# Who issues the copies of the second half of x: GpSimd in the source's order, or SP

## The chip, the cores and the metric

The kernel runs on one core of a Trainium2 chip. The core has five engines with an instruction stream each: TensorE (PE; its weight loads are shown as PEld), VectorE (DVE), ScalarE (ACT), GpSimd (POOL) and SyncE (SP), which only issues transfers. Transfers (DMAs) are issued by SP, ScalarE or GpSimd and carried out by 16 DMA engines that all of them share. The metric is device time in microseconds (us), the median of several runs; less is better.

## The reference, cut to what matters

Two layers of graph attention on x, 8 batches of 2048 nodes with 256 channels (float32), with one adjacency matrix of 2048 x 2048 integers. About one entry in 128 is set, and the diagonal always is, so a node has some 17 neighbours on average. After each layer the input is added and the rows are normalised.

```python
# layer 0, for each batch
h1, h2, h3 = x @ W1, x @ W2, x @ W3
e = leaky_relu(h1 @ h2.T, 0.2)
e = where(adj > 0, e, -1e12)
x = layernorm(x + relu(softmax(e) @ h3))
# layer 1, for each batch; q has 4 heads of 64 channels
q = x @ W
e = leaky_relu(e_src[:, None, :] + e_dst[None, :, :], 0.2)   # q against the vector a
e = where(adj > 0, e, -9e15)
x = layernorm(x + elu(softmax(e over the neighbours) @ q))
```

## The kernel before, in words

The kernel uses that the matrix is sparse. It never forms the 2048 x 2048 logits. It makes a list of neighbours for every node and gathers the neighbours' rows.

**Tables.** The 8 batches are two halves of four. For each half there is a table in DRAM, `xg[0]` and `xg[1]`, of 2048 rows with the four batches side by side (1024 floats, 4 KB a row), so that one gather by node number fetches the row of all four batches. The table is made by transfers from DRAM to DRAM: for `xg[0]` by four of 2 MB (L255), for `xg[1]` by eight of 1 MB (L955), each for half the nodes of one batch. A row of such a transfer is 1 KB.

**Setup.** SP loads the adjacency matrix in 16 pieces. VectorE numbers the set entries, SP writes them back to DRAM as `edges`; in the midst of this it issues the four transfers of `xg[0]`. The nodes are ranked by degree, so that each tile of 128 nodes has its own number of slots (neighbour places): `SLOTS`, from 12 to 38.

**Units.** A unit is one tile of one half in one layer. Layer 0 takes the 16 tiles of half 0 and then those of half 1, each from 12 slots up to 38; layer 1 has 32 units more. A unit of layer 0 has these steps:

- `list_job` gathers a tile's rows of `edges` (tile `nb`, 1 MB), and `neighbours` takes the neighbour numbers out of them on VectorE (MAX8 and MATCH_REPLACE8, L491 and L494); done once for each tile, during half 0;
- `before0` gathers the tile's own rows (`xo`), copies them (`xr`, by SP, L512) and makes `g` of them: transposes on TensorE, copies `xT` on ScalarE (L407), a projection on TensorE, copies `g` on ScalarE (L523);
- `chunk_job` gathers the neighbours' rows, one indirect DMA of 128 rows for a slot, two slots to a ring tile `s` (L191);
- `logits0` multiplies each row with `g` and sums on VectorE (L543, four for a slot), then the softmax;
- `sums0` scales the rows on ScalarE (L634, four for a slot) and adds them on TensorE (L612, four for a slot);
- `after0` projects, normalises and writes the row of layer 1's table (`qg`).

**Order.** Two things set it. The loop at the end of `fast_path` writes the program: for each unit it goes through the slots of `sums0`, and at each slot `tick` first lets `pump` issue gathers as long as ring tiles are free (`credits`, `RING` = 16), then moves the logits of later units, the list of a later tile and the ends of earlier units on by a step. After that a planner orders the instructions of each engine by its own costs and by what they wait for. From L339 on GpSimd is taken out of this (`manual_schedule`): its instructions stay in the order in which the source writes them. SP's don't: the planner may put a transfer of SP as early as its data allow. The eight transfers of `xg[1]` stand in the loop at the starts of the units 2 to 9 (L952 to L955).

An engine works through its stream in order: an instruction that waits holds up all behind it. The first instructions that read `xg[1]` are the gathers of unit 16.

Of the kernel before, what the change touches and what calls it, by code (L numbers as in the profile page):

```python
# [125 lines left out]
def fast_path(  # L126
# [24 lines left out]
    nc = tc.nc  # L151
    B, N, C = x.shape
    NT = N // P
    KC = C // P
    HB = B // 2
# [51 lines left out]
    xg = [tc.dram_tile([N, HC], F32, name=f"xg_{h}") for h in range(2)]  # L207
# [273 lines left out]
    def neighbours(t):  # L481
        K, o = SLOTS[t], offs[t]
        while t not in loaded:
            yield
        v = loaded[t]
        if t in up[:3]:
            numbered(v)
        rounds = -(-K // 8)
        m = sp.tile([P, 40], F32, tag="m", name=f"m_{t}")
        for i in range(rounds):  # L490
            nc.vector.max(m[:, ts(i, 8)], v)  # L491
            yield
            if i + 1 < rounds:
                nc.vector.match_replace(v, m[:, ts(i, 8)], v, 0.0)  # L494
                yield
        credits[0] += 1
        nc.vector.tensor_scalar(neg[:, o : o + K], m[:, :K], 0.5, LOWEST, ALU.is_lt, ALU.mult)
        far = sp.tile([P, 40], F32, tag="far", name=f"far_{t}", bufs=2)[:, :K]
        nc.vector.tensor_scalar(far, m[:, :K], 0.5, FAR, ALU.is_lt, ALU.mult)
        nc.vector.scalar_tensor_tensor(  # L500
            idx[:, o : o + K], m[:, :K], 1.0, far, ALU.subtract, ALU.add
        )
        listed[t] = True
# [416 lines left out]
    def finish(u):  # L920
        yield from after[u.layer](u)
# [6 lines left out]
    def tick(limit):  # L928
        pump()
        while late and late[0][0] <= clock[0]:  # L930
            late.popleft()[1]()
        for _ in range(2):
            if ahead[0] < limit:
                ahead[0] += next(stream, 0)
        for queue in queues:
            for _ in range(min(len(queue), 2)):
                if queue and next(queue[0], queue) is queue:
                    queue.popleft()
        clock[0] += 1
# [6 lines left out]
    for j, u in enumerate(units):  # L946
        begun = False
        if 0 < j and j + 2 < NT:
            lists.append(neighbours(up[j + 2]))
        while len(ends) > 1:  # L950
            tick(0)
        if 2 <= j < 10:  # L952
            b, half = divmod(j - 2, 2)
            n = ts(half, N // 2)
            nc.sync.dma_start(xg[1][n, ts(b, C)], x[HB + b, n])  # L955
        left = float(u.K)
        for share in sums[u.layer](u):
            ahead[0] -= share
            left -= share
            tick(left + units[min(j + 1, len(units) - 1)].K + LEAD)  # L960
            if not begun and left <= u.K / 2 and j + 3 < len(units):
                begun = True
                v = units[j + 3]
                starts.append(before[v.layer](v))
        ends.append(finish(u))
# [249 lines left out]
@with_exitstack  # L1215
def kernel(
    ctx: ExitStack,
    tc: tile.TileContext,
    x: bass.AP,
    adj: bass.AP,  # L1220
    w1: bass.AP,
    w2: bass.AP,
    w3: bass.AP,
    wq: bass.AP,
    a: bass.AP,
    out: bass.AP,
):
    nc = tc.nc
    flagp = ctx.enter_context(tc.tile_pool(name="flag", bufs=1))
    flag = flagp.tile([1, 1], I32, tag="flag", name="flag")  # L1230
    fast_path(tc, x, adj, w1, w2, w3, wq, a, out, flag)
    again = nc.values_load(
        flag, min_val=0, max_val=1, skip_runtime_bounds_check_because="a comparison gave it"
    )
    with tc.If(again > 0):
        general_path(tc, x, adj, w1, w2, w3, wq, a, out)
# [29 lines left out]
```

## Time and profile before

| what | before |
|---|---|
| median of three runs | 2865.22 us (2856.55 to 2866.15) |
| the profiled execution's own time | 2741.96 us |
| its span, first to last instruction | 2740.1 us |
| busy: PE, DVE, ACT, POOL | 1857.8, 2270.1, 1827.9, 1515.4 us |
| transfers of `xg[1]` (L955) | 8 of 1024 KB, issued by SP from 99.3 to 155.9 us |
| gathers of layer 0 (`s<-xg,idx`) | 602, from 126.4 to 1676.3 us, 1014 ns each (median) |
| logits of layer 0 (L543) | 2408 of 424 ns on DVE |
| scaling of rows, layer 0 (L634) | 2408 of 506 ns on ACT |

The profile is of one execution, which was shorter than the timed runs. A timeline row gives the start, the time taken, the engine, the line, the operation, what is written and read, how many instructions of a kind are put together, and, in brackets, how long the engine stood idle before it and what ended that. A row of SP has a "q": issuing is the work of its queue, and the time is that of the issue, not of the transfer. A GpSimd row of an indirect DMA is the time in which its descriptors are written; the rows land later.

### The profile page before, as it was taken

The page shows a single profiled execution, that of the slowest core. Times are in us where ns is not written, and L with a number is a line of the kernel's source. Part 1 is how long each engine was busy: PE and PEld are TensorE (multiplying, and loading weights), DVE is VectorE, ACT ScalarE, POOL GpSimd, SP SyncE. Part 2 cuts the span into 40 slices and gives each one's busy share as a digit, 9 for nine tenths or more (in the row PEclk, how much of TensorE's full clock was granted, in tenths as well). Part 3 has the DMA queues.
Part 4 walks back from the last instruction along what each step waited for, and adds up shares of the span by engine and source line. Part 5 has one row for each costly group of instructions (what it writes and reads, how often), then busy time and mean ns, then how long its engine had stood idle before and what let it go on. Part 6 is the DMA issues. An engine that isn't in the chain of part 4 may idle for free. (4 is left out here: it accounts for less than half of the span.)

```text
span 2740.1 us, 42566 instructions
## 1 busy us (share of the span) xinstructions
PE 1857.8 (68%) x12003; PEld 792.3 (29%) x12003; DVE 2270.1 (83%) x7247; ACT 1827.9 (67%) x4937; POOL 1515.4 (55%) x1506
## 2 busy tenths in 40 slices
PE   0148888888786866686878767756656667655763
PEld 0124434333332333343434323312221222211221
DVE  7679999999987876777787786788888888888996
ACT  6137787878879986867878779644445555554454
POOL 1353454545444544544454545577767777777773
PEclk9569999999988988898988888877877878877876
DMA  9996776777765566767686774899789998997892
GB/s 388 380 376 207 270 262 245 260 245 263 261 221 200 183 215 215 252 212 268 219 277 217 242 263 154 287 332 357 268 315 354 348 344 317 358 351 269 305 354 89
DMA packets 248036, 749.51 MB, mean 274 GB/s; under 512 B 55712, under 2 KB 73248, under 8 KB 241648
## 3 DMA queue, kind: packets, MB, share of 16 engines
q0 software_dynamic: 192064, 644.32, 66.5%
q1 hardware_dynamic: 54464, 101.21, 10.4%
q8 instruction: 98, 1.61, 0.2%
q10 hardware_dynamic: 1264, 1.18, 0.1%
q14 instruction: 146, 1.20, 0.1%
HBM read 721.50 MB, written 84.48 MB: 294 GB/s over the span
## 5 line engine op out<-in xcount | busy, mean ns | idle before, releaser
L612 PE MATMUL acc<-s,ident 64*64 64x512 f32 x9632 | 1336.4, 653 | 469.0 <-issue 285.4
L543 DVE CUSTOM_DVE_ANT_0 j<-s,g 128x256 bf16<-128x256 f32 x2408 | 1019.9, 424 | 199.1 <-DMA s<-xg,idx 133.0
L191 POOL DMA_INDIRECT s<-xg,idx x602 | 632.4, 1051 | 771.7 <-ACT s L634 280.9
L634 ACT ACTIVATE s<-s,e 128x256 f32<-128x256 f32 x2408 | 1000.1, 506 | 28.3 <-DVE e L569 27.4
L191 POOL DMA_INDIRECT s<-qg,idx x602 | 614.8, 1021 | 233.4 <-issue 123.7
L612 PEld LDWEIGHTS acc<-s,ident 64*64 64x64 f32 x9632 | 391.1, 144 | 1211.5 <-issue 777.6
L813 DVE TENSOR_TENSOR s<-s,p 128x2048 f32<-128x2048 f32 (+1 forms) x262 | 577.5, 2222 | 0.0
L809 ACT ACTIVATE s<-s,e 128x64 f32<-128x64 f32 x1472 | 357.8, 335 | 47.1 <-DVE e L777 35.8
L543 DVE DVE_READ_ACCUMULATOR2_ANT e<- 128x1 f32 x2408 | 197.0, 82 | 0.0
L696 PE MATMUL ps_q<-wqs,x1T 128*128 128x264 f32 x512 | 147.7, 426 | 35.9 <-ACT x1T L407 25.1
L199 POOL DMA_INDIRECT out_dram<-o,oidx x128 | 130.2, 1017 | 71.5 <-ACT o L395 36.7
L405 PE MATMUL ps_t_x<-ident,xo 128*128 128x128 f32 x256 | 56.7, 365 | 162.7 <-DMA xo<-xg,order 162.6
L383 ACT ACTIVATE z<-mv,roots 128x4 f32<-128x4 f32 x64 | 19.0, 297 | 212.2 <-DVE mv L373 212.1
L747 DVE TENSOR_TENSOR e<-s,own 128x32 f32<-128x32 f32 (+1 forms) x312 | 56.9, 186 | 104.0 <-DMA s<-qg,idx 97.6
L415 PE MATMUL ps_p_g<-A,xT 128*128 128x256 f32 x512 | 129.4, 399 | 8.9 <-DVE so L705 5.2
L415 PE MATMUL ps_p_h<-w_sb,hT 128*128 128x256 f32 x512 | 127.8, 392 | 1.4 <-ACT hT L407 1.4
L696 PEld LDWEIGHTS ps_q<-wqs,x1T 128*128 128x128 f32 x512 | 100.8, 206 | 88.4 <-ACT x1T L407 32.8
L395 ACT ACTIVATE o<-xr,nmr,rstd 128x256 f32<-128x256 f32 x128 | 66.3, 589 | 76.9 <-DVE nmr L391 67.3
L415 PEld LDWEIGHTS ps_p_g<-A,xT 128*128 128x128 f32 x512 | 96.7, 196 | 53.2 <-ACT s L634 8.1
L763 ACT ACTIVATE e<-e 128x304 f32<-128x304 f32 (+11 forms) x34 | 14.9, 439 | 143.7 <-DVE e L762 143.7
L491 DVE MAX8 m<-nb 128x8 f32<-128x2048 f32 x44 | 100.5, 2286 | 11.9 <-DMA nb<-edges,order 11.7
L415 PEld LDWEIGHTS ps_p_h<-w_sb,hT 128*128 128x128 f32 x512 | 92.0, 189 | 63.3 <-issue 17.9
(130 smaller groups left out, 1486.2 us busy)
## 6 DMA issues: line engine op xcount, KB each, us to landing
adj<-in_adj_dram SPq DMA_DIRECT2D x16, 1024.0 KB, 8.9
edges<-adj SPq DMA_DIRECT2D x16, 1024.0 KB, 19.8
xr<-xo SPq DMA_DIRECT2D x128, 128.0 KB, 6.9
x1s<-y SPq DMA_DIRECT2D x32, 512.0 KB, 7.3
xr<-x1s SPq DMA_DIRECT2D x32, 512.0 KB, 6.9
s<-xg,idx POOLq DMA_INDIRECT x602
s<-qg,idx POOLq DMA_INDIRECT x602
xg<-in_x_dram SPq DMA_DIRECT2D x4, 2048.0 KB
```

Source lines behind the costliest of these rows:

```text
L191: nc.gpsimd.indirect_dma_start(out=dst, out_offset=None, in_=table, in_offset=AT(ap=index, axis=0), bounds_check=table.shape[0] - 1, oob_i ...
L199: ins = nc.gpsimd.indirect_dma_start(out=table, out_offset=AT(ap=index, axis=0), in_=src, in_offset=None)
L395: nc.scalar.activation(dst[:, b, :], y[:, b, :], AF.Identity, bias=nmr[:, b : b + 1], scale=rstd[:, b : b + 1],)
L415: nc.tensor.matmul(pp[:, ts(j, C)], lhsT=srcT[:, ts((2 * i + j) * KC + k, P)], rhs=weight[:, k, :], start=(k == 0), stop=(k == KC - 1),)
L491: nc.vector.max(m[:, ts(i, 8)], v)
L543: nc.vector.tensor_tensor_reduce(out=jt, in0=rows[:, s, ts(b, C)], in1=u.g[:, ts(b, C)], scale=1.0, scalar=0.0, op0=ALU.mult, op1=ALU.add, ...
L612: nc.tensor.matmul(acc[r][64 * c : 64 * c + 64, :], lhsT=ident[rr, rr], rhs=rows[rr, s, c * 2 * w_ : (c + 1) * 2 * w_].rearrange("p (j w) ...
L634: nc.scalar.activation(v, v, AF.Copy, scale=u.p[i][:, b, k : k + 1])
L696: nc.tensor.matmul(pq[:, : C + 2 * H], lhsT=x1T[:, ts(i * KC + k, P)], rhs=w.wqs[:, k, :], start=(k == 0), stop=(k == KC - 1),)
L747: nc.vector.tensor_tensor(e[:, c * CHUNK : c * CHUNK + ns, :].rearrange("p s (b g) -> p s b g", b=HB), rows[:, :ns, :].rearrange("p s (b w ...
L809: nc.scalar.activation(v[:, a, g, :], v[:, a, g, :], AF.Copy, scale=pv[:, a, g : g + 1])
L813: nc.vector.tensor_tensor(v, v, pv.unsqueeze(3).to_broadcast([P, n * HB, H, D]), ALU.mult)
```

## The change

The eight transfers are issued by GpSimd instead of by SP. Their place in the source, their sizes, sources and destinations stay. GpSimd's instructions keep the source's order, so the transfers stand among its gathers where the loop writes them.

```diff
@@ -952,7 +952,8 @@
         if 2 <= j < 10:
             b, half = divmod(j - 2, 2)
             n = ts(half, N // 2)
-            nc.sync.dma_start(xg[1][n, ts(b, C)], x[HB + b, n])
+
+            nc.gpsimd.dma_start(xg[1][n, ts(b, C)], x[HB + b, n])
         left = float(u.K)
         for share in sums[u.layer](u):
             ahead[0] -= share
```

## The prediction

> **What bounds the kernel now.** I read the page first: the slices of each engine, then the DMA row.
>
> ```profile
> span 2740.1 us, 42566 instructions
> ...
> DVE  7679999999987876777787786788888888888996
> ...
> DMA  9996776777765566767686774899789998997892
> ```
>
> A slice is 68.5 us. The DMA engines are full in the first three; from the fourth on (205 us) VectorE is at 90% or more up to 750 us. So VectorE sets the pace of the first half of layer 0, and the start is another regime. The engines' busy time by stretch shows where one ends:
>
> ```profile
> 99.00:190.00 91.00, 20.98 (x71) 13.21 (x72) 63.72 (x141) 16.61 (x39) 40.78 (x40) 0.56 1.04 392
> 190.00:245.00 55.00, 45.73 (x254) 22.05 (x254) 50.76 (x222) 36.76 (x89) 24.71 (x23) 0.90 0.72 239
> 245.00:560.00 315.00, 269.06 (x1440) 127.25 (x1436) 304.23 (x1202) 245.96 (x603) 147.53 (x142) 0.94 0.73 254
> ```
>
> (Columns: stretch, length, busy time of PE, weight loads, DVE, ACT, POOL, then granted clock, DMA share, GB/s.) Up to 190 us the DMA share is 1.04; from 245 to 560 us it is 0.73 while DVE is busy 304 of 315. The changed transfers lie in the full stretch. This is SP's queue there:
>
> ```profile
> 99.30 41.97 SPq L955 DMA_DIRECT2D xg<-in_x_dram  x6
> 141.36 13.86 SPq L512 DMA_DIRECT2D xr<-xo  x4
> 155.26 12.06 SPq L955 DMA_DIRECT2D xg<-in_x_dram  x2
> ```
>
> All eight are issued between 99 and 168 us, long before their first reader (unit 16, whose first gather is at 801.8 us). What that costs VectorE is in its timeline:
>
> ```profile
> 154.66 2.29 DVE L491 MAX8 m<-nb 128x8 f32<-128x2048 f32 x1 [1.72 <-DMA nb<-edges,order]
> ...
> 180.31 2.29 DVE L491 MAX8 m<-nb 128x8 f32<-128x2048 f32 x1 [8.86 <-DMA nb<-edges,order]
> ...
> 190.24 0.43 DVE L543 CUSTOM_DVE_ANT_0 j<-s,g 128x256 bf16<-128x256 f32 x1 [2.92 <-ACT g L523]
> ...
> 192.63 0.43 DVE L543 CUSTOM_DVE_ANT_0 j<-s,g 128x256 bf16<-128x256 f32 x1 [1.38 <-ACT g L523]
> ```
>
> With 1.92 us before its first row of s at 136.64, VectorE idles 16.8 us between 121 and 193 us. After that, up to 560 us, its waits for DMAs add up to 0.2 us. So a microsecond saved on VectorE before 193 us moves all that follows, and the 16.8 us are all that can be had there.
>
> **What the Trainium skill says.** "DMA: Bandwidth & Descriptors", section "Issuing engines are not separate DMA queues": DMAs from any engine share the same 16 DMA engines. The trace agrees: with SP's transfers beside them, a gathered list issued at 166.50 is read only at 180.31, against 7.2 us from issue to use at 343.06. So the bytes don't get cheaper by moving; only their time of day changes. Same page, "Anatomy of one DMA": descriptor generation on GpSimd is "small, variable". No row of before has a plain DMA on POOL, so it can't be compared. "SBUF — State Buffer", section "SBUF: two separate sides": GpSimd can be locked out of writing descriptors by some VectorE operations; in the trace the gathers of rows stay near their median of 1014 ns (2240 at most), so I add nothing for it.
>
> **The change, part by part.**
>
> *Removed from SP:* eight issues, 54 us of SP's time (41.97 + 12.06); nothing that VectorE needs soon stands behind them. The copies xr<-xo that follow are read at 220 us; they come earlier, for no gain.
>
> *Removed from the DMA engines at 121 to 190 us:* 8 x 1 MiB. Between 121 and 131 us, when little else moves, the rate is 331 GB/s, so one transfer is 3.2 us of all engines and eight are 25.3 us. Step by step, with the order on the engines as it is:
>
> (a) The first row of s lands before VectorE is free (134.72): -1.92. (b) The list at 154.66: its 1.72 go too; together -3.64. (c) The list at 180.31:
>
> ```profile
> 166.50 1.08 POOL L191 DMA_INDIRECT nb<-edges,order  x1 [0.32 <-DMA s<-xg,idx]
> 168.11 0.99 POOL L191 DMA_INDIRECT xo<-xg,order  x1 [0.53 <-DMA s<-xg,idx]
> ...
> 343.06 1.02 POOL L191 DMA_INDIRECT nb<-edges,order  x1 [6.47 <-PE acc L612]
> ```
>
> POOL waited about 3.3 us for its own earlier gathers just before, so the list is issued near 163 and lands 7.2 us later, at 170, ten earlier. But VectorE then waits for g of unit 1, and that is set by ScalarE:
>
> ```profile
> 171.54 10.47 ACT L634 ACTIVATE s<-s,e 128x256 f32<-128x256 f32 x26 [0.77 <-DMA s<-xg,idx]
> 183.16 0.59 ACT L407 COPY xT<-ps_t_x 128x512 f32<-128x512 f32 x1 [1.15 <-PE ps_t_x L405]
> ...
> 189.62 0.59 ACT L523 COPY g<-ps_p_g 128x512 f32<-128x512 f32 x1 [3.02 <-PE ps_p_g L415]
> ```
>
> The 26 scalings end at 182.01 - 3.64 = 178.4. The copy xT, in order behind them, starts then and not at 183.16 (PE's transposes are done by then: xo lands near 172): -4.8. From there to g nothing changes (projection on PE, 6.5 us). So L543 of unit 1 starts some **5 us** earlier. That is what I take for the gain; it is bounded by 3.64 (if xo is no earlier) and 16.8 (if the planner, seeing other times, puts xT ahead of the scalings).
>
> *Added to POOL:* eight plain DMAs, in the source's order. Following the loop's credits and clock through the source gives POOL's order; it agrees with all 1,444 gathers and scatters of the two layers in the trace. By it the transfers stand after the instructions that end at 245, 285, 331, 371, 413, 463, 509 and 553 us. Cost of one on POOL: from below 1.0 us (a gather's row, 128 descriptors), from above 8 us (1,024 rows of 1 KB, eight times as many). I take 4. The cover: behind each, within five instructions, POOL idles waiting for ring buffers (12.05, 12.3, 6.5 and 4.0, 9.3, 11.7, 7.6, 7.5, 5.5 and 8.8 us), and in units 3 to 10 a gather ends at least 12 us, mostly over 20, before VectorE reads its row. A landing takes 4 to 7 us, so 8 us on POOL and 3.2 us of data are hidden: 0. Were both covers gone, they would cost 8 x (4 + 3.2) = 58 us.
>
> One place has no cover. The first transfer stands two instructions ahead of a list:
>
> ```profile
> 247.05 1.09 POOL L191 DMA_INDIRECT nb<-edges,order  x1 [0.30 <-ACT hs L647]
> ...
> 256.30 2.29 DVE L491 MAX8 m<-nb 128x8 f32<-128x2048 f32 x1
> ```
>
> From issue to use are 9.2 us, to landing some 7.4: 1.9 us to spare. The transfer adds its time on POOL with the gap of 0.3 and what of its 3.2 us of data isn't overlapped: 4.5 us (POOL 1.0) to about 8 (POOL 8). VectorE loses 2.6 to 6; or 0, if the planner, which knows POOL's new order, places that step later. At 343.06 and 166.50 too the step stands just behind the landing, so it seems to follow POOL's issue; I take 0 and keep 6 for the range.
>
> *Added to the DMA engines at 245 to 560 us:* 25.3 us in 315, so their share goes from 0.73 to 0.81: room. Each transfer goes through POOL's own queue, so gathers behind it wait 3.2 us; covered as above. POOL waits for the DMA eight before: a transfer has over 9 us (seven gathers of 1.3) to land. The gathers of unit 16 wait for the transfers, the last of which is done some 240 us before.
>
> *Sum:* -5 + 0 = -5, against the profiled execution's 2741.96 us (span 2740.1), 2737. The median of the runs is 2865.22, 4.5% more; scaled, -5 stays -5: **2860**.
>
> **The rivals.**
>
> *The whole stall goes.* For it: DMA share 1.04 exactly where VectorE idles. Against: ScalarE's 26 scalings stand ahead of xT. All 16.8 us, times 1.045: 2848.
>
> *Another order.* Only POOL's order is fixed; DVE, ACT, PE and SP follow a planner's costs. It gets other times for SP and POOL, and may order the rest otherwise to the end. Sensitive is the second half of layer 0 (913 to 1684 us), where rows arrive just in time: VectorE waits 115.8 us for s, PE 123.6 us for xo. A quarter of either is some 30 us: 2835 or 2895; half as much, 2850 or 2880, is as likely.
>
> *Slower: POOL's writing of descriptors.* From 245 to 560 us POOL is busy 147.5 us, and 142 gaps of 0.3 add 43: some 124 us are free for eight transfers, 15.5 each. Above that POOL is the bound; the lead of 12 to 20 us delays it by two units or so. At 25 us each, 8 x 9.5 = 76, less a lead of 17: +59, 2924. It decides from 16 us up. Against: that is twice the proportional price.
>
> *It doesn't move.* If POOL's transfers were placed at the start as SP's were, the time would stay 2865; POOL's order being the source's speaks against it.
>
> **How the numbers follow.** Small gain or none, as summed: 0.42. The whole stall gone: 0.19. Another order: 0.31 (faster 0.16, slower 0.11, near nothing 0.04). POOL bound: 0.06. Not moved: 0.02. A measurement tells about 0.5% (14 us) from no change. The stall gone counts as faster (17 us), so faster 0.35, same 0.48, slower 0.17. The likeliest case's own range is 2850 to 2868 (its gain from 3.64 to the 16.8 that bound it, less up to 6 for the list, and the 0.1% by which medians may differ); 8 in 10 takes in the stall gone and most of the reorderings: 2828 to 2884.
>
> **What would show it.** Right: no 1 KB traffic of SP after 99 us; the DMA share below 0.95 from 131 to 190 us; the two list waits (1.72, 8.86) gone; the first L543 of unit 1 near 185; eight plain DMAs on POOL from about 240 to 550 us; VectorE still 96% busy between. Wrong: a POOL row above 16 us, VectorE waiting for s or nb there, or, with the start 5 us earlier and these stages alike, a changed length of the stretch from unit 16 on: then the order did it.

## The result and the profile after

| kernel | median | range, runs |
|---|---|---|
| before | 2864.71 us | 2856.55 to 2869.58, 20 |
| after | 2864.61 us | 2857.77 to 2870.38, 20 |

The ratio is 1.0001, with a 95% interval from 0.9992 to 1.0009 (-2.3 to +2.6 us): no change that can be measured. The 5 us forecast did not come.

One thing has to be known for all that follows: the same kernel takes a different time on different occasions, 2741 to 2743 us on some and 2845 to 2865 us on others, and the profile on which the prediction was made belongs to the first kind, while the timing above and the profile after belong to the second. So each kernel is compared only with the kernel before timed on the same occasion, and for a like-for-like profile of both kernels the first experiment is used.

The page of the kernel after, by slices of 71.7 us:

```profile
span 2867.7 us, 42563 instructions
...
DVE  7668899998987876767787875777777678877886
...
DMA  9986787878665666677776757886788889887883
```

The third slice of the DMA row went from 9 to 8, and the sixth to eighth from 7, 6, 7 to 8, 7, 8: the bytes have moved to a later time. The engines' busy time by stretch in the kernel after (columns as before: PE, weight loads, DVE, ACT, POOL, then granted clock, DMA share, GB/s) says how much:

```profile
99.00:190.00 91.00, 16.18 (x61) 9.73 (x61) 63.40 (x141) 13.11 (x32) 41.31 (x41) 0.56 0.83 305
190.00:245.00 55.00, 46.05 (x253) 22.75 (x254) 45.84 (x195) 37.82 (x91) 21.28 (x21) 0.94 0.62 209
245.00:560.00 315.00, 265.22 (x1384) 124.35 (x1384) 295.52 (x1197) 241.91 (x593) 151.85 (x147) 0.92 0.77 269
```

From 1.04 to 0.83 in the stretch at the start, and from 0.73 to 0.77 after 245 us. Yet VectorE did no more work by 190 us than before (63.40 against 63.72 us busy), and less between 245 and 560 us (295.52 against 304.23). SP's queue in the kernel after has no 1 MiB transfer left there; only the copies xr<-xo follow the loading of the edges:

```profile
91.22 5.34 SPq L252 DMA_DIRECT2D edges<-adj  x3
121.02 106.39 SPq L512 DMA_DIRECT2D xr<-xo  x16
```

The instructions that touch x, in the kernel after (durations in ns, least, median and most, then the first and the last start):

```profile
L956 POOL DMA_DIRECT2D xg<-in_x_dram x8: 830/846/850, 249.2 to 566.4; - x8
```

Eight transfers on GpSimd, 0.85 us of its time each. And VectorE's timeline of the kernel after, in unit 0 and at the first logits of unit 1:

```profile
164.64 0.43 DVE L543 CUSTOM_DVE_ANT_0 j<-s,g 128x256 bf16<-128x256 f32 x1 [1.93 <-remote]
...
168.17 0.43 DVE L543 CUSTOM_DVE_ANT_0 j<-s,g 128x256 bf16<-128x256 f32 x1 [1.65 <-remote]
...
172.60 0.43 DVE L543 CUSTOM_DVE_ANT_0 j<-s,g 128x256 bf16<-128x256 f32 x1 [1.80 <-issue]
...
193.41 0.42 DVE L543 CUSTOM_DVE_ANT_0 j<-s,g 128x256 bf16<-128x256 f32 x1 [7.09 <-ACT g L523]
```

The two waits for lists (1.72 and 8.86 us) are gone, as forecast. But 11 logits of unit 0 now start late, by 0.2 to 1.9 us each, 11.8 us together. No DMA is named behind them; the rows of s that they read had landed by 147 us, and other logits of the same rows ran without a gap. "issue" and "remote" say that the profile shows no instruction of this core for which they waited; in the other six the row names only the VectorE instruction just before. I call them **late starts**. With them unit 0's logits end at 177.5 us (169.5 before), and unit 1 begins at 193.41 us instead of 190.24.

### The profile page after: what moved, and what is told of

Same layout as the page of the kernel before. It is cut to its first block, busy times and chain, and to the rows that moved or that the text cites. A ratio compares the mean times of both kernels' runs of the same rounds, so it can differ in the third digit from the quotient of the medians.

```text
span 2867.7 us, 42563 instructions
## 1 busy us (share of the span) xinstructions
PE 2106.8 (73%) x12003; PEld 902.8 (31%) x12003; DVE 2275.1 (79%) x7247; ACT 1833.3 (64%) x4937; POOL 1515.5 (53%) x1514
## 4 chain that ended last, share of the span: by engine, by line
PE 29%; DVE 26%; issue 17%; DMA 13%; ACT 10%; POOL 3%; another core or an unknown queue 1%; POOLq 0%; SPq 0%; DVEq 0%; ACTq 0%
PE acc L612 23%; DVE j L543 12%; ACT s L634 8%; DMA s<-xg,idx 4%; DMA s<-qg,idx 3%; DVE s L813 3%; DMA xo<-xg,order 3%; POOL s L191 3%; DVE m L491 2%; DVE e L543 2%; DVE nb L494 1%; PE ps_q L696 1%; PE ps_t_x L405 1%; PE ps_p_h L415 1%
## 5 line engine op out<-in xcount | busy, mean ns | idle before, releaser
L612 PE MATMUL acc<-s,ident 64*64 64x512 f32 x9632 | 1584.3, 667 | 372.9 <-issue 217.2
L612 PEld LDWEIGHTS acc<-s,ident 64*64 64x64 f32 x9632 | 499.2, 146 | 1247.7 <-issue 953.2
L415 PEld LDWEIGHTS ps_p_g<-A,xT 128*128 128x128 f32 x512 | 95.3, 194 | 53.4 <-ACT xT L407 10.4
L405 PEld LDWEIGHTS ps_t_x<-ident,xo 128*128 128x128 f32 x256 | 36.7, 180 | 209.1 <-issue 187.8
```

What stands on the lines that cost most here:

```text
L405: nc.tensor.transpose(pt[:, ts(j, P)], src[:, ts(4 * i + j, P)], ident)
L415: nc.tensor.matmul(pp[:, ts(j, C)], lhsT=srcT[:, ts((2 * i + j) * KC + k, P)], rhs=weight[:, k, :], start=(k == 0), stop=(k == KC - 1),)
L612: nc.tensor.matmul(acc[r][64 * c : 64 * c + 64, :], lhsT=ident[rr, rr], rhs=rows[rr, s, c * 2 * w_ : (c + 1) * 2 * w_].rearrange("p (j w) ...
```

## The experiments

All kernels were timed against the kernel before on the same occasion. The order of the instructions on PE, DVE and ACT in the kernel after is, instruction by instruction, that of the kernel before; the same holds for all kernels below but the one with doubled transfers on POOL, where a few of the 7,247 DVE instructions stand elsewhere.

| occasion | before (runs) | kernel | ratio | 95% interval |
|---|---|---|---|---|
| A | 2864.71 (20) | after | 1.0001 | 0.9992 to 1.0009 |
| B | 2742.57 (26) | before again | 1.0007 | 0.9998 to 1.0017 |
| B | | after | 0.9970 | 0.9958 to 0.9982 |
| B | | transfers left out | 0.9967 | 0.9954 to 0.9980 |
| B | | transfers twice, on SP | 1.0091 | 1.0078 to 1.0104 |
| C | 2861.52 (50) | late on SP | 1.0025 | 1.0015 to 1.0035 |
| C | | one unit later on POOL | 0.9987 | 0.9978 to 0.9996 |
| C | | transfers twice, on POOL | 1.0013 | 1.0003 to 1.0024 |
| D | 2845.32 (33) | transfers left out | 0.9999 | 0.9988 to 1.0011 |
| D | | one unit later on POOL | 0.9970 | 0.9958 to 0.9983 |
| D | | late on SP | 1.0007 | 0.9996 to 1.0019 |
| E | 2741.00 (11) | after | 0.9975 | 0.9962 to 0.9987 |

**Both kernels again (occasion B).** No edit.

> The kernel before once more, for a profile beside the others' and for what two timings of one kernel differ by. Every theory: ratio to before 1.000, within 0.001. If the 2741.96 us of the first profile was particular to that execution, this profile's own time is near 2865 us; the idle time of VectorE in 99 to 193 us is then read anew, and the 8.86 us wait for a list and the 1.72 us one should stand again.

> The changed kernel once more, on the same chip as the kernel before. Theory 1 (VectorE's idle time at the start is only refilled by something later in the same stretch, so nothing is gained and nothing is given back): ratio 1.000 within 0.001, first L543 of unit 1 at 190 us or later. Theory 2 (5 us are gained at the start and given back between 245 and 560 us): ratio 1.000, first L543 of unit 1 near 185 us, and VectorE about 5 us less busy than before's in 245 to 560 us.

The kernel after is faster here: 0.9970, that is 8.3 us (4.9 to 11.5). VectorE's timeline of the kernel before on this occasion:

```profile
158.56 2.29 DVE L491 MAX8 m<-nb 128x8 f32<-128x2048 f32 x1 [2.26 <-DMA nb<-edges,order]
...
181.54 2.30 DVE L491 MAX8 m<-nb 128x8 f32<-128x2048 f32 x1 [6.15 <-DMA nb<-edges,order]
...
189.41 0.43 DVE L543 CUSTOM_DVE_ANT_0 j<-s,g 128x256 bf16<-128x256 f32 x1 [0.85 <-ACT g L523]
```

And of the kernel after:

```profile
170.36 2.29 DVE L491 MAX8 m<-nb 128x8 f32<-128x2048 f32 x1 [2.87 <-DMA nb<-edges,order]
...
182.70 0.43 DVE L543 CUSTOM_DVE_ANT_0 j<-s,g 128x256 bf16<-128x256 f32 x1 [5.32 <-ACT g L523]
...
250.45 2.29 DVE L491 MAX8 m<-nb 128x8 f32<-128x2048 f32 x1 [2.25 <-DMA nb<-edges,order]
```

Neither has a late start in unit 0. Three things can be read. The second list is read at 170.36 us and not at 181.54. What holds VectorE then is g of unit 1, by 5.32 us, so the logits of unit 1 start 6.7 us earlier (7.5 against the first profile's 190.24) and not 11. And a list at 250.45 us makes VectorE wait 2.25 us where the kernel before had no wait. The cause of that wait stands in POOL's timeline of the kernel after:

```profile
237.15 0.85 POOL L956 DMA_DIRECT2D xg<-in_x_dram  x1
238.30 1.23 POOL L191 DMA_INDIRECT s<-xg,idx  x1 [0.30 <-PE ps_t_x L405]
239.83 1.06 POOL L191 DMA_INDIRECT nb<-edges,order  x1 [0.31 <-ACT x1T L407]
```

The list is two instructions behind the first transfer. It is used 10.6 us after its issue; in the kernel without transfers (below) 9.3 us were enough, without a wait.

ScalarE's timeline of the kernel after shows why g comes when it does:

```profile
167.57 10.48 ACT L634 ACTIVATE s<-s,e 128x256 f32<-128x256 f32 x26 [0.77 <-DVE e L569]
177.96 1.04 ACT L407 COPY xT<-ps_t_x 128x512 f32<-128x512 f32 x2
178.90 2.10 ACT L634 ACTIVATE s<-s,e 128x256 f32<-128x256 f32 x5
182.08 0.58 ACT L523 COPY g<-ps_p_g 128x512 f32<-128x512 f32 x1 [1.07 <-PE ps_p_g L415]
```

The 26 scalings stand ahead of xT, and xT starts the moment they end: 177.96 us, 5.2 earlier than in the first profile. Both copies of xT now follow each other, and g is copied 4.1 us after xT's start instead of 6.5. Against the first profile both things help. The kernel before on this occasion had the second of them already:

```profile
175.47 10.48 ACT L634 ACTIVATE s<-s,e 128x256 f32<-128x256 f32 x26 [0.78 <-DVE e L569]
185.86 1.04 ACT L407 COPY xT<-ps_t_x 128x512 f32<-128x512 f32 x2
```

Its g follows 3.0 us after xT. So what was gained here came from ahead of the scalings: the waits for the first row of s (4.3 us in this profile of before) and for the first list (2.26). The 6.15 us at the second list ran beside ScalarE's chain, which would have held unit 1 up anyway.

By the units' logits the lead is 6.7 us at the start of unit 1, 4.2 at the start of unit 4 (286.22 against 290.46), 4.7 at the start of unit 10 and 6.1 at the end of layer 0 (1679.0 against 1685.1). The rest of the 8.3 us is within what two executions of layer 1 differ by: 1053.9 in this profile of before, 1056.3 in the first one, 1049.9 in this one of after. So of the first two theories the second is right in kind, and wrong in that less is given back than gained.

**The transfers left out (occasion B).** The table of half 0 serves for both halves.

```diff
-    xg = [tc.dram_tile([N, HC], F32, name=f"xg_{h}") for h in range(2)]
+    xg = [tc.dram_tile([N, HC], F32, name="xg_0")] * 2
...
-            nc.sync.dma_start(xg[1][n, ts(b, C)], x[HB + b, n])
+            pass
```

> The eight transfers are left out altogether, and both halves read the one table, so half 1 of the output is computed from half 0's rows; all other instructions stay in their order. Theory 1: the transfers cost nothing in either place, ratio 1.000 within 0.001. Theory 2: the gain of the start without the price after it, 5 us less than before, ratio 0.998. The rival of the prediction in which the whole stall goes: 17 us less, ratio 0.994.

0.9967, or 9.1 us (5.5 to 12.6): as much as the kernel after, within the intervals. VectorE's timeline of this kernel:

```profile
168.85 2.29 DVE L491 MAX8 m<-nb 128x8 f32<-128x2048 f32 x1 [1.73 <-DMA nb<-edges,order]
...
181.14 0.43 DVE L543 CUSTOM_DVE_ANT_0 j<-s,g 128x256 bf16<-128x256 f32 x1 [5.28 <-ACT g L523]
```

With no transfer at all, unit 1 starts only 1.6 us earlier than in the kernel after, and g still costs 5.28 us. With this order of instructions that is what any placing of the transfers can bring at the start: some 8 us, not the 16.8 us of VectorE's idle time. At the end of layer 0 it leads by 7.8 us, the kernel after by 6.1.

**Each transfer twice, on SP (occasion B).** The second copy goes into a table that nobody reads.

```diff
-    xg = [tc.dram_tile([N, HC], F32, name=f"xg_{h}") for h in range(2)]
+    xg = [tc.dram_tile([N, HC], F32, name=f"xg_{h}") for h in range(3)]
...
-            nc.sync.dma_start(xg[1][n, ts(b, C)], x[HB + b, n])
+            [nc.sync.dma_start(xg[k][n, ts(b, C)], x[HB + b, n]) for k in (1, 2)]
```

> As the kernel before, but each of the eight transfers is issued twice by SP, the second time into a table that nobody reads: 16 MiB at the start in place of 8, some 25 us more of all DMA engines. If the DMA time at the start reaches the end of the kernel one for one, ratio 1.009 (25 us); if it does so only for what ScalarE's scalings don't cover (the 5 us of the prediction are the same again), 5 to 15 us, 1.002 to 1.005. Theory 1, with room still left at the start: ratio 1.000 within 0.001.

1.0091, or 25 us (21 to 29): the eight added transfers cost as much as the 25 us that their bytes take, while leaving out the first eight saved 9. VectorE's timeline of this kernel, at unit 2:

```profile
238.65 2.29 DVE L491 MAX8 m<-nb 128x8 f32<-128x2048 f32 x1 [24.64 <-DMA nb<-edges,order]
```

The list that VectorE needs at 214 us comes 24.64 us late. Why, SP's queue and POOL's timeline show:

```profile
161.29 50.58 SPq L955 DMA_DIRECT2D xg<-in_x_dram  x10
212.38 33.16 SPq L512 DMA_DIRECT2D xr<-xo  x12
```

```profile
224.31 0.99 POOL L191 DMA_INDIRECT xo<-xg,order  x1 [30.70 <-DMA xr<-xo]
...
230.79 0.99 POOL L191 DMA_INDIRECT nb<-edges,order  x1 [0.30 <-ACT xT L407]
```

SP's ten later transfers are issued until 212 us, and the copies xr<-xo stand behind them in SP's queue. POOL's next gather of xo waits 30.70 us for such a copy, and the list stands behind that gather in POOL's order. Once issued, it is read 7.9 us later, as fast as elsewhere. So the added transfers do reach the end of the kernel, but by the queue that they share with the copies; what 8 MiB more would cost at the start with nothing behind them in their queue was not run. In the kernel before on this occasion POOL waits 0.3 us for such a copy.

**The kernel before once more (occasion C).** No edit; one profile.

> A further profile of the kernel before. If it takes about 2742 us, it is the same as the earlier profile, L543 of unit 1 starting at 189 to 190 us and unit 3 ending near 290 us. If it takes about 2865 us, as both kernels did where the change was first timed, it decides between two readings of why nothing was gained there: either VectorE's stalls within unit 0 (11.3 us of waits without a cause on this core, in 99 to 330 us of the changed kernel's profile) stand in this kernel too, and unit 1 starts some 7 us later than in the changed kernel (near 200 us); or they don't, and it starts at about 190 us, which is no later than the 193.4 us of the changed kernel.

This one took 2859.62 us. VectorE's timeline of the kernel before on this occasion:

```profile
180.59 2.29 DVE L491 MAX8 m<-nb 128x8 f32<-128x2048 f32 x1 [9.31 <-DMA nb<-edges,order]
...
190.48 0.43 DVE L543 CUSTOM_DVE_ANT_0 j<-s,g 128x256 bf16<-128x256 f32 x1 [2.88 <-issue]
```

The second reading holds: unit 1 starts at 190.48 us, no later than the 193.41 us of the kernel after. There are no late starts in unit 0 here (there are in unit 3, 5.6 us), while the lists' waits stand, 1.77 and 9.31 us. The two waits together are 11.1 us, about what the late starts of unit 0 take in the kernel after (11.8).

**The transfers left out, where the kernel is slower (occasion D).** Same edit as above.

> The eight transfers left out again, both halves reading the one table, so half 1 of the output is computed from half 0's rows. Where the kernel before takes about 2742 us: 0.997 again, unit 1 starting near 181 us. Where it takes about 2861 us, the theory that VectorE's own late starts take the place of the waits for the lists says: the transfers cost nothing there at the start, ratio 0.999 to 1.001, unit 1 starting no earlier than 187 us, with 5 to 12 us of late starts inside unit 0. The rival, that POOL's transfers give back between 245 and 560 us what was gained: 0.996 or less there too, unit 1 starting near 181 us.

0.9999 (-3.4 to +3.1 us), where the same edit had saved 9.1 us on occasion B. VectorE's timeline of this kernel on occasion D:

```profile
163.32 0.42 DVE L543 CUSTOM_DVE_ANT_0 j<-s,g 128x256 bf16<-128x256 f32 x1 [0.96 <-DVE e L543]
...
166.14 0.43 DVE L543 CUSTOM_DVE_ANT_0 j<-s,g 128x256 bf16<-128x256 f32 x1 [0.97 <-DVE e L543]
...
170.79 0.20 DVE L566 TENSOR_REDUCE s<-e 128x4 f32<-128x48 f32 x1 [0.92 <-issue]
171.94 0.18 DVE L568 RECIPROCAL s<-s 128x4 f32<-128x4 f32 x1 [0.95 <-DVE s L566]
172.65 0.21 DVE L569 TENSOR_TENSOR e<-e,s 128x48 f32<-128x48 f32 x1 [0.53 <-DVE s L568]
...
186.88 0.42 DVE L543 CUSTOM_DVE_ANT_0 j<-s,g 128x256 bf16<-128x256 f32 x1 [7.10 <-ACT g L523]
```

Five logits of unit 0 start late, 3.9 us together, and six steps of its softmax too, some 3.1 us more than usual: 7.0 us, within the 5 to 12 expected. The softmax ends at 172.9 us, 5.7 later than without the transfers on occasion B (167.1), and from there to unit 1 it is 14.0 us in both. So unit 1 starts at 186.9 us, near the 187 named, and 3.6 us before the 190.5 of occasion C, not 8. With the transfers gone there is nothing that POOL could give back, and still nothing is gained. So a price of the transfers' new place is not needed to explain why nothing was gained when the change was first timed. It is not excluded to the microsecond: on this same occasion another kernel, below, gained 8.5 us for a reason that I don't know, so differences of that size between kernels are not all understood there.

**The transfers late, but on SP (occasions C and D).** Each waits for a 1 KB transfer of POOL into its own rows.

```diff
+            nc.gpsimd.dma_start(xg[1][half * (N // 2) : half * (N // 2) + 1, ts(b, C)], x[HB + b, half * (N // 2) : half * (N // 2) + 1])
             nc.sync.dma_start(xg[1][n, ts(b, C)], x[HB + b, n])
```

> The transfers stay on SP, but each waits for a 1 KB transfer of POOL into its own rows of the table, put where the changed kernel has its transfer; so SP moves the same bytes at the changed kernel's times. If only the time of day counts: 0.997 of the kernel before, as the changed kernel has, with L543 of unit 1 near 183 us, and unit 3 as long as in the changed kernel (43.0 us from its first L543 to its last). If POOL's queue counts, because gathers behind the transfer wait for its 3.2 us: unit 3 is 40.6 us, as in the kernel before, and 2 to 3 us more are gained. If the issuing engine is what gains: 1.000.

> SP moves the bytes at the changed kernel's times, as before. Where the kernel before takes about 2742 us: 0.996 to 0.997 if only the time of day counts; 1.000 if the issuing engine is what gains; above 1.001 if the wait that now stands in SP's queue holds up the copies behind it. Where it takes about 2861 us: 1.0025 again.

1.0025 and 1.0007. Both runs fell on occasions of the slower kind (on D leaving the transfers out gained nothing; on C it wasn't tried), so they can't tell whether the issuing engine or the time of day gains. That rival stays untested. Unit 3 takes 47.1 and 46.5 us against 47.6 in the kernel before, with late starts in each. No list waits near 250 us, which fits the reading that the wait comes from the transfer ahead of the list in POOL's own queue; but late starts would hide such a wait here. Why occasion C shows 7 us more I could not find: the profiled execution took 2863.0 us, 7 less than the median of 2870.05.

**One unit later on POOL (occasions C and D).**

```diff
-        if 2 <= j < 10:
-            b, half = divmod(j - 2, 2)
+        if 3 <= j < 11:
+            b, half = divmod(j - 3, 2)
```

> The changed kernel with the eight transfers one unit later (units 3 to 10 in place of 2 to 9), so that the first is no longer ahead of the list of 247 us, which has little lead over its reader. If that list gives back 2.4 us: unit 3 is 40.6 us long again and the ratio to before is 0.996 (2 us less than the changed kernel). If any list behind a transfer gives it back: as the changed kernel, 0.997, and the 2.4 us are found in unit 4.

> The changed kernel with the transfers one unit later, as before. Where the kernel before takes about 2742 us: if the list near 247 us gave back 2.4 us, unit 3 is 40.6 us long and the ratio 0.996; if any list behind a transfer does, 0.997 with the 2.4 us in unit 4. Where it takes about 2861 us: 0.9987 again.

0.9987 and 0.9970. Unit 3 takes 48.5 and 46.6 us, with 6.6 and 5.1 us of late starts inside, so the 2.4 us can't be seen in it. The gain (3.7 and 8.5 us) has no place in the start: unit 1 starts at 192.4 and 188.7 us, no earlier than without transfers. It is larger than that of leaving the transfers out on the same occasion, and I don't know where it comes from. It is the only kernel that was faster than before on occasions of the slower kind, by 0.1 and 0.3%; it wasn't run where the kernel before takes 2742 us.

**Each transfer twice, on POOL (occasion C).**

```diff
-            nc.sync.dma_start(xg[1][n, ts(b, C)], x[HB + b, n])
+            [nc.gpsimd.dma_start(xg[k][n, ts(b, C)], x[HB + b, n]) for k in (1, 2)]
```

(with a third table, as on SP.)

> The changed kernel with every transfer issued twice by POOL, the second time into a table that nobody reads: 16 MiB between 245 and 560 us. If the lead of the gathers covers it, as the prediction has it: 3 us more at the list of unit 3 and no more elsewhere, 0.998 of the kernel before. If transfers there cost their 3.2 us one for one, as they did at the start: 25 us more than the changed kernel, 1.006.

1.0013, or 3.7 us (0.9 to 6.9), between the two expectations. Both counted on a changed kernel at 0.997, which occasions of this kind don't show (1.0001 on A); against 1.000, 25 us are refuted and a few are not. This kernel's stretch from 245 to 560 us, and the list behind the first two transfers:

```profile
245.00:560.00 315.00, 269.05 (x1417) 127.00 (x1416) 297.12 (x1177) 244.61 (x600) 154.36 (x152) 0.94 0.85 295
```

```profile
259.34 2.29 DVE L491 MAX8 m<-nb 128x8 f32<-128x2048 f32 x1 [3.02 <-DMA nb<-edges,order]
```

16 MiB in 315 us take the DMA share to 0.85, and VectorE is as busy as in the kernel after (295.52). From the start of unit 4 to the end of unit 10 it takes 317.6 us, the kernel after 318.5 and the kernel before on this occasion 318.5; on occasion B it is 317.2 in the kernel after and 317.5 before. So transfers there are free, the list apart.

**The kernel after a third time (occasion E).** No edit.

> The changed kernel once more. Where the kernel before takes about 2742 us: 0.997 again. Where it takes 2845 to 2870 us, the theory that VectorE's late starts take the place of the waits removed says 0.999 to 1.001, with 3 to 12 us of late starts inside unit 0; a ratio of 0.998 or less there says that the first timing's 1.0001 was particular to it.

0.9975, or 6.9 us (3.6 to 10.4), where the kernel before takes 2741.00 us. Unit 1 starts at 180.9 us, no late start, and the list near 248 us waits 1.26 us. The chip was that of occasion D, some six minutes later; so it isn't the chip that makes the difference of 100 us.

## Why the prediction was right or wrong

**The number.** 2864.6 us lies within the range of 2828 to 2884 and inside that of the likeliest case. That says little for the mechanism: a forecast of -5 us in 2865 and no gain at all can't be told apart by this range. The mechanism came true on occasions B and E, where it gained 8.3 and 6.9 us; on the occasion of the timing nothing was gained, and the 4.6 us by which 2860 misses are nearly the whole forecast gain. To that extent it is luck that the number lies where it should. (The foot of the likeliest range, 2850, is also above the prediction's own bound: 2865.2 - 16.8 is 2848.)

**The bound.** Right. VectorE is busy for 302 of the 315 us from 245 us in the kernel after of occasion B, and what is gained before stays to the end of layer 0.

**What leaves the start.** Right on occasions B and E: row of s without a wait and first list with none or 0.5 us, second list read at 170.36 us where the prediction said it lands at 170, then g of unit 1 as the next bound. The size was a little off: 6.7 to 8.5 us against 5. Against the profile that the prediction was made on, the term that failed is "from there to g nothing changes": 4.1 us from xT to g, not 6.5, because the second half of xT no longer waits for its transposes. Against the kernel before on the same occasion it is the two early waits, 6.6 us where the first profile had 3.64. The rival in which the whole 16.8 us go is refuted: even without transfers unit 1 starts only 8 to 9 us earlier. The sign "DMA share below 0.95 from 131 to 190 us" held in the first profile after (0.86), not on occasion B (0.97, from 1.04): there gathers pulled forward fill it, and without any transfer it is 0.98. That DMAs of all engines share the same 16, as the Trainium skill says in "DMA: Bandwidth & Descriptors", section "Issuing engines are not separate DMA queues", agrees with occasion B: POOL's second list was read 12.8 us after its issue with SP's transfers beside it (168.77 to 181.54) and 7.9 us without (162.51 to 170.36). That nothing VectorE needs soon stands behind the transfers in SP's queue held for occasion B; with the transfers doubled, the copies behind them are what cost 25 us, and on occasion C POOL waits 9.2 us for them in the kernel before.

**The cost on POOL.** 0.85 us and not 4; the lower bound, 1.0, was still too high. A plain transfer of 1,024 rows costs POOL less than a gather of 128 (1.0 us), so the price doesn't follow the rows. The places were right within the shift of the profile, and the slower rival (16 us or more each) falls.

**The list at 247 us.** The choice of 0 was wrong. It rested on "if the planner places that step later", and the planner changed nothing on PE, DVE or ACT. It costs 2.25 and 1.26 us with one transfer ahead, below the range given (2.6 to 6), and 3.02 with two. The cover elsewhere was right.

**Another order.** Refuted, with its 0.31.

**From the profile to the runs.** This is the step that failed: "scaled, -5 stays -5". It took the runs of 2865 us for the profile's 2742 us, stretched evenly. They are another regime, at the start too. There VectorE starts late in unit 0 once it no longer stops for a list: all seven profiles of such occasions without the waits show it, 5.8 to 11.8 us in unit 0, and unit 1 starts at 186.9 to 193.4 us in them. The one profile there of the kernel before, which stops, shows none in unit 0, and starts unit 1 at 190.5. On occasion B the sum of the steps (-6.7 at unit 1, +2.25 at the list, so -4.5) is close to the -4.2 us seen at unit 4; on occasion A the median is 0. So the late starts stand where the waits were. What brings them on, and that they account for the missing microseconds one for one, is not shown: at the end of layer 0 single profiles there differ by up to 16 us (1697.3 to 1713.0), more than the effect, and the kernel with the transfers one unit later was faster in spite of them. The rival of this kind, a wait that takes the place of the one removed, had been considered only for POOL and the planner.

## What to carry to other kernels

Bulk transfers are cheap in a stretch in which gathers have a lead: here 16 MiB there left the kernel at most 7 us above the kernel before. Taking 8 MiB out of the full stretch gained 7 to 9 us on occasions B and E and nothing dependable on the others. Look also at what stands behind a transfer in its own queue and who waits for that: 8 MiB more on SP cost 25 us through small copies behind them. Of an engine's idle time only as much comes back as the next bound leaves, so look for what it waits for next, and for a reader with little lead right behind the new place. And ask whether the profile was taken under the conditions of the timed runs: when its own time lies outside their range, a few microseconds read from it may not be there in them.

## What the runs showed of the hardware that was not expected

The same kernel takes 2741 to 2743 us or 2845 to 2865 us, by occasion; one chip showed both. The pages of the kernel before on occasion B:

```profile
PE 1856.9 (68%) x12003; PEld 793.7 (29%) x12003; DVE 2270.5 (83%) x7247; ACT 1827.9 (67%) x4937; POOL 1511.1 (55%) x1506
```

and on occasion C:

```profile
PE 2111.9 (74%) x12003; PEld 910.4 (32%) x12003; DVE 2273.7 (80%) x7247; ACT 1835.2 (64%) x4937; POOL 1508.8 (53%) x1506
```

PE shows 255 us more for the same 12,003 matmuls, the other engines at most 7 us, and the granted clock is no lower (0.854 against 0.846). A single matmul of L612, the most frequent line, took hardly longer (664 ns against 653 on average), so they overlap less. Most of the 119 us of span is in layer 1: 1157.5 against 1053.9 us. And starts that wait for nothing that the profile shows appear on ScalarE; its chief waits of that kind on occasion C, where on B there are none:

```profile
ACT s L809 <- issue: 48.4, 56, 4.1
ACT e L763 <- issue: 36.9, 7, 10.7
```

(total, times, longest, in us.) On VectorE such waits add up to 66 us on C and 6 us on B. Up to 330 us, VectorE's late starts on the slower occasions fall into the same stretches of its instructions: the end of unit 0, the second half of unit 2, and unit 3 (in the kernel before into unit 3 alone). The packets that bring instructions took as long on both kinds of occasion (1.03 us on C and 1.07 on B, a packet of 16 KB), so slower fetching of a packet is not the cause. Whether packets came too late is not known, and what the cause is stays open.
